# Merging du * B on GpSimd, and moving two pieces of a selective-scan pipeline

## The chip, the cores and the metric

The kernel runs on one core of one Trainium2 chip. The core has five instruction streams that work side by side and meet through semaphores: TensorE (PE; the profile keeps the loading of its stationary operand apart as PEld), VectorE (DVE), ScalarE (ACT), GpSimd (POOL) and SyncE (SP, which issues the DMAs here). The metric is device time in microseconds for one execution of the whole program. A profiled execution also gives the span from the first to the last instruction.

## The reference

Four images of 64 x 64 pixels and 96 channels go through four layers. Layers 0 and 1 are state-space layers and hold nearly all of the time; layers 2 and 3 are linear attention and a quantised feed-forward on the tokens. Layer 1 works on the Fourier transform of the image (33 columns instead of 64). The core of layers 0 and 1 is the same selective scan over four directions, with 16 states for each channel:

```python
def step(hst, inputs):
    ul, dl, bl, cl = inputs
    dA = jnp.exp(dl[..., None] * A)
    hst = hst * dA + (dl * ul)[..., None] * bl[:, :, None, :]
    y = jnp.einsum('bkdn,bkn->bkd', hst, cl)
    return (hst, y)
```

Here `dl` is delta and `dl * ul` is du. For each state n the kernel needs exp(delta * A[n]), the product du * B[n], the running recurrence h, and the sum over n of h * C[n].

## The kernel before

**Tiles.** 128 channels lie on the partitions, and time lies along the free dimension. A layer has three such channel chunks (C = 3). Time is cut into segments of at most 512 columns: eight of 512 in layer 0; 512, 512, 384, 384 and 320 in layer 1. Layer 0 takes two images at once and runs two phases (one for each pair of images) of 4 directions x 8 segments; layer 1 runs four phases (one for each image) of 4 x 5 segments.

**Steps.** A segment is 12 steps: four groups q of four states each, times three chunks c. That makes 2 x 32 x 12 = 768 steps in layer 0 and 4 x 20 x 12 = 960 in layer 1, 1728 in all. One step makes four scans, j = 0 to 3, one for each state of its group. The work is spread over the engines like this:

- For j = 0 and 1 the product du * B is made on ACT in transposed form (bx, L646) and turned by PE into a PSUM bank (`transposed`, L678). The decay exp(delta * A) comes from ACT into SBUF (`front_x`, L682).
- For j = 2 and 3 the product is made on POOL (`front_b`, L700), from du and a tile of B that DMA has spread over the partitions, into places 1 and 2 of a tile h of three states. The decay comes from ACT into a PSUM bank (`front_y`).
- DVE runs the four scans (`scan`, L710). Scan 0 writes into PSUM, over its own input; scans 1 and 2 write into places 0 and 1 of h. Scan 3 writes into place 2 of h, or, in steps whose `kept` holds 3, into PSUM over its decay.
- A state that was kept in PSUM is multiplied by C on DVE into a tile hk (`multiply_kept`, L728), and its last column is put into the state by ACT (`keep_state`, L735). The states in h, two or three, are multiplied by C on POOL in one instruction (`multiply`, L747), after a copy of their last columns (L744).
- PE adds all products into acc, a PSUM bank for each chunk, by transposing them with accumulation (`accumulate`, L757; `add_kept` for hk, `add_rest` for h). After the last group ACT copies acc out (`close_chunk`, L788).

**Order.** The loop over steps writes every engine's order by hand, and each engine runs its own instructions strictly in that order. During step i (called `st`) PE adds the h of step i-2 (`older`), POOL multiplies the h of step i-1 (`before`) and then makes du * B for step i+1 (`nxt`), and PE transposes for step i+1. In `slot` pieces of other work are put in: the preparation of the next segment (`prepare`: projections, delta, du on POOL in L604) and side tasks (projection, convolution, gating, output projection and Fourier transforms of other images; the token layers).

**Buffers that tie the engines.** h has three buffers, so du * B for step i+1 goes into the buffer of step i-2 and waits until PE has added it. The PSUM banks for decays and transposes (`room`) go round by three, in the order: decay 2, decay 3, transposes 0 of the next step, transposes 1 of the next step. So transposes 0 wait for the bank that scan 1 has read, and transposes 1 for the one that scan 2 has read. hk has two buffers, B and C two each.

Of the kernel before, what the change touches and what calls it, by code (L numbers as in the profile page):

```python
# [11 lines left out]
ALU = mybir.AluOpType  # L12
# [10 lines left out]
C, P = 3, 128  # L23
# [7 lines left out]
class Cfg:  # L31
# [5 lines left out]
    def __init__(self, pre, NI, KI, NR, nat, R, parts, rows, segs, eps):  # L37
        self.pre = pre
        self.NI, self.PI, self.KI = NI, P // NI, KI
        self.DI = C * self.PI  # L40
        self.NR, self.L, self.nat = NR, NR * 64, nat
        self.R, self.M = R, R + 2 * NST
        self.parts = parts
        self.rows = [(sum(rows[:i]), n) for i, n in enumerate(rows)]
        self.segs = [(sum(segs[:i]), n) for i, n in enumerate(segs)]
        self.eps = eps
# [466 lines left out]
class Step:  # L513


    def __init__(self, z, q, c):
        self.z, self.q, self.c = z, q, c
        self.nm = f"{z.nm}_{q}_{c}"
        self.kept = (0, 3) if (C * q + c) % (2 * z.cfg.KI) == 1 else (0,)
        self.hk = {}  # L520
        self.px, self.ay = {}, {}


def scans(tc, ctx, phases, ident):
# [8 lines left out]
    nc = tc.nc  # L533
# [96 lines left out]
    def fetch_b(z, q):  # L630
        z.b[q] = broadcast(z, 4 * q + 2, 2, 0)

    def fetch_c(z, q):
        z.c[q] = broadcast(z, 4 * q, 4, 1)

    def make_bx(z, q):

        NI, PI, M, R = z.cfg.NI, z.cfg.PI, z.cfg.M, z.cfg.R
        for j in range(2):
            t = sp.tile([P, NBK, C, P], F32, name=f"bx_{z.nm}_{q}_{j}", tag="bx", bufs=4)  # L640
            z.bx[q, j] = t
            for b, (_, n) in enumerate(z.blocks):
                for i in range(NI):
                    m = i * M + R + 4 * q + j
                    ch = slice(i * PI, (i + 1) * PI)
                    nc.scalar.activation(  # L646
                        t[:n, b, :, ch], z.dut[:n, b, :, ch], AF.Copy, scale=z.bt[:n, b, m : m + 1]
                    )
                    yield
# [15 lines left out]
    def drain(gen):  # L665
        for _ in gen:
            pass
# [3 lines left out]
    def room(st, j):  # L671
        return ps.tile([P, 512], F32, name=f"ab_{st.nm}_{j}", tag=f"ab{next(turn) % 3}")

    def transposed(st, j):

        pb = st.px[j] = room(st, j)
        for b, (t, n) in enumerate(st.z.blocks):
            nc.tensor.transpose(pb[:, t : t + n], st.z.bx[st.q, j][:n, b, st.c], ident[:n, :n])  # L678
# [7 lines left out]
    def front_x(st):  # L686
        st.ax = sp.tile([P, 2, SM], F32, name=f"ax_{st.nm}", tag="ax", bufs=2)
        for j in range(2):
            exp(st.ax[:, j, : st.z.S], st, 4 * st.q + j)
# [5 lines left out]
    def front_b(st):  # L695

        S = st.z.S
        st.h = sp.tile([P, 3, SM], F32, name=f"h_{st.nm}", tag="h", bufs=3)
        for j in range(2):
            nc.gpsimd.tensor_tensor(  # L700
                st.h[:, 1 + j, :S], st.z.du[:, st.c, :S], st.z.b[st.q][:, j, :S], ALU.mult
            )

    def scan(st, j):
        z = st.z
# [43 lines left out]
    def accumulate(st, hc, first=False, last=False):  # L749
        z = st.z  # L750
        if first:
            z.acc[st.c] = ps.tile([P, 512], F32, name=f"acc_{z.nm}_{st.c}", tag=f"acc{st.c}").rearrange(
                "p (b d) -> p b d", b=NBK
            )
        blocks = list(enumerate(z.blocks))
        for b, (t, m) in blocks[:: -1 if last else 1]:
            nc.tensor.matmul(  # L757
                z.acc[st.c][:m, b, :],
                hc[:, t : t + m],
                ident,  # L760
                start=(first and b == 0),
                stop=(last and b == 0),
                is_transpose=True,
            )
# [6 lines left out]
    def add_kept(st, j):  # L771
        accumulate(st, st.hk[j], first=(st.q == 0 and j == 0))
# [26 lines left out]
    with tc.manual_schedule(engines=IN_ORDER):  # L799
        drain(prepare(segs[0]))  # L800
        drain(make_bx(segs[0], 0))
        fetch_b(segs[0], 0)
        fetch_c(segs[0], 0)
        st = steps[0]
        for j in range(2):
            transposed(st, j)
        front_x(st)
        front_b(st)
        before = older = None
        more, pgen, pwants, at, due = Pieces(segs[0], 1, 4), none, None, 0, 0.0  # L810

        def prepare_more(kind):

            nonlocal pwants
            if pwants not in (None, kind):
                return False
            pwants = next(pgen, LATE)
            return True

        def slot(kind, hold=False):  # L820


            nonlocal due
            if hold:
                E.flush()
                return
            prepare_more(kind)
            due = min(due + st.z.ph.rate / 3, 3.0)
            for _ in range(min(int(due), 1 + (due >= 2.0))):
                due -= E.step(kind)  # L830

        def burst():

            if BURST in (pwants, E.wants):
                E.flush()
            if pwants is BURST:
                return prepare_more(BURST)
            if E.wants is BURST:
                E.step(BURST)
                return True  # L840
            return False

        for i, st in enumerate(steps):
            z, q, c, S = st.z, st.q, st.c, st.z.S
            nxt = steps[i + 1] if i + 1 < len(steps) else None
            if q == 0 and c == 0:
                after = z.after
                fresh = at == 0 or z.ph is not segs[at - 1].ph
                if fresh:
                    z.ph.io["y"] = [z.blk.dram_tile(f"y{j}", (2, z.cfg.L, C * P), z.ph.g) for j in range(2)]  # L850
                open_segment(z, segs[at - 1] if at else None)
                if after:
                    E.require(after.ph.needs[after.k % 2])
                pgen, pwants = prepare(after) if after else none, None
                at += 1
            if fresh and q == 0 and c == C - 1:
                for fn, arg in z.ph.side:
                    E.add((fn, arg), fn(E, arg))
            if c == 0:
                if q + 1 < NQ:  # L860
                    fetch_b(z, q + 1)
                elif after:
                    drain(pgen)
                    more = Pieces(after, 0, 4)
                    fetch_b(after, 0)
            if c == 1:
                if q + 1 < NQ:
                    fetch_c(z, q + 1)
                elif after:
                    fetch_c(after, 0)  # L870
            if older:
                add_rest(older)
            if before and 3 in before.kept:
                keep_state(before, 3)
                add_kept(before, 3)
            scan(st, 0)
            front_y(st, 2)
            if nxt:
                front_x(nxt)
            multiply_kept(st, 0)  # L880
            keep_state(st, 0)
            add_kept(st, 0)
            front_y(st, 3)
            long = burst()
            if before:
                multiply(before)
            if nxt:
                front_b(nxt)
            scan(st, 1)
            if nxt:  # L890
                if c == C - 1:
                    drain(more.gen)
                    if q + 2 < NQ:
                        more = Pieces(z, q + 2, 6)
                    elif q + 1 == NQ:
                        more = Pieces(nxt.z, 1, 6)
            slot(None)
            if nxt:
                transposed(nxt, 0)
            more.take(skip=long)  # L900
            scan(st, 2)
            slot(None, hold=long)
            if nxt:
                transposed(nxt, 1)
            if older and older.q == NQ - 1:
                close_chunk(older)
            scan(st, 3)
            if 3 in st.kept:
                multiply_kept(st, 3)
            more.take(skip=long and c == C - 1)  # L910
            slot(LATE)
            older, before = before, st
        multiply(before)
        if 3 in before.kept:
            add_kept(before, 3)
        for st in (older, before):
            add_rest(st)
            close_chunk(st)
        E.finish()
# [704 lines left out]
```

## Time and profile before

| what | value |
|---|---|
| median of 3 runs | 11189.63 us (11177.26 to 11195.26) |
| the profiled execution | 11196.25 us |
| its span | 11194.5 us |
| instructions | 162858 |
| mean granted TensorE clock | 0.901 |
| DMA, read and written | 1215.67 MB and 236.50 MB |

The median and the profiled execution are different runs, so a sum made from the profile's rows belongs to the second and third of these times. A row of the groups gives the line, the engine, the operation, output <- inputs, the shape and the number of instructions; then the busy time in us and the mean duration of one in ns; then the idle time of that engine just before them and what ended it. Lines such as L700 are lines of the kernel before. Names of tiles have their numbers left out: `ab_l` and `b_l` are banks of `room`, `k_l` and `hk_l` are hk, `bc_l` is a spread tile of B or C.

### The profile page before, as it was taken

How to read it: one execution, taken by the hardware profiler on the slowest of the kernel's cores; microseconds unless marked ns; L12 is line 12 of the kernel's file. 1: busy time of each engine (PE TensorE's matmuls, PEld its weight loads, DVE VectorE, ACT ScalarE, POOL GpSimd, SP SyncE). 2: the span in 40 equal slices, each digit the busy share in tenths (PEclk: the TensorE clock that was granted, in tenths of full speed). 3: DMA queues.
4: the chain of work that ended last, by engine and by line, in shares of the span. 5: the costliest groups of instructions: out<-in, count | busy, mean ns of one | idle time of the engine just before them, and what ended most of it. 6: DMA issues, size and time to landing. Idle time of an engine off the chain costs nothing.

```text
span 11194.5 us, 162858 instructions
## 1 busy us (share of the span) xinstructions
PE 8922.4 (80%) x54560; PEld 6578.7 (59%) x54560; DVE 9751.5 (87%) x10419; ACT 9340.7 (83%) x19428; POOL 9616.7 (86%) x7464
## 2 busy tenths in 40 slices
PE   5668788777888888888988888887778877886766
PEld 2555555555667666656775565665556655665554
DVE  5889999889998998999788778988988989889874
ACT  3779999998888998998778878888888888888864
POOL 2999999988888998999789889998988889889870
PEclk8889999889898998999889989998889888999887
DMA  5655554655666546555544444542345322542242
GB/s 145 144 133 124 132 133 121 156 152 150 159 157 136 140 128 149 132 144 161 156 132 130 142 129 128 176 133 88 99 130 146 104 89 97 171 120 93 85 137 44
DMA packets 1204409, 1462.83 MB, mean 131 GB/s; under 512 B 478134, under 2 KB 1017848, under 8 KB 1145072
## 3 DMA queue, kind: packets, MB, share of 16 engines
q1 hardware_dynamic: 1203567, 1452.41, 48.0%
q8 instruction: 431, 7.06, 0.3%
q14 instruction: 411, 3.36, 0.1%
HBM read 1215.67 MB, written 236.50 MB: 130 GB/s over the span
## 4 chain that ended last, share of the span: by engine, by line
POOL 31%; PE 23%; ACT 20%; DVE 16%; issue 7%; DMA 2%; SPq 1%; POOLq 0%; DVEq 0%; ACTq 0%
POOL h_l L747 14%; POOL h_l L700 12%; DVE h_l L710 7%; PE acc_l L757 6%; ACT bx_l L646 4%; ACT ax_l L682 4%; ACT b_l L682 3%; DVE b_l L710 2%; DVE ab_l L710 2%; PE b_l L678 2%; PE pc_l L297 2%; POOL du_l L604 2%; PE pp_l L571 1%; PE pi_l L210 1%; ACT ab_l L682 1%
## 5 line engine op out<-in xcount | busy, mean ns | idle before, releaser
L747 POOL TENSOR_TENSOR h_l<-h_l,bc_l 128x1536 f32<-128x1536 f32 (+2 forms) x1728 | 4783.3, 2768 | 176.1 <-DVE h_l L710 56.1
L700 POOL TENSOR_TENSOR h_l<-du_l,bc_l 128x512 f32<-128x512 f32 (+2 forms) x3456 | 3970.6, 1171 | 582.4 <-PE acc_l L757 552.4
L646 ACT ACTIVATE bx_l<-dut_l,bt_l 128x192 f32<-128x192 f32 (+2 forms) x6272 | 2755.1, 499 | 0.3
L757 PE MATMUL acc_l<-ident,h_l 128*128 128x128 f32 (+1 forms) x16656 | 2427.3, 299 | 293.1 <-POOL h_l L747 291.6
L757 PEld LDWEIGHTS acc_l<-ident,h_l 128*128 128x128 f32 (+1 forms) x16656 | 2129.2, 154 | 901.1 <-POOL h_l L747 469.9
L682 ACT ACTIVATE ax_l<-delta_l,l_alog 128x512 f32<-128x512 f32 (+2 forms) x3456 | 2140.7, 667 | 0.0
L710 DVE TENSOR_TENSOR_SCAN h_l<-b_l,state_l,h_l 128x512 f32<-128x512 f32 (+2 forms) x1386 | 1506.4, 1109 | 132.8 <-ACT b_l L682 113.6
L678 PE MATMUL b_l<-ident,bx_l 128*128 128x128 f32 (+1 forms) x6874 | 1211.8, 295 | 220.4 <-DVE h_l L710 213.4
L682 ACT ACTIVATE b_l<-delta_l,l_alog 128x512 f32<-128x512 f32 (+2 forms) x1968 | 1231.7, 626 | 120.1 <-DVE h_l L710 47.4
L678 PEld LDWEIGHTS b_l<-ident,bx_l 128*128 128x128 f32 (+1 forms) x6874 | 857.1, 149 | 799.9 <-DVE h_l L710 465.8
L710 DVE TENSOR_TENSOR_SCAN b_l<-ax_l,state_l,b_l 128x512 f32<-128x512 f32 (+2 forms) x851 | 965.3, 1134 | 227.8 <-PE b_l L678 225.7
L678 PE MATMUL ab_l<-ident,bx_l 128*128 128x128 f32 x5312 | 888.7, 296 | 228.0 <-DVE h_l L710 220.6
L682 ACT ACTIVATE ab_l<-delta_l,l_alog 128x512 f32<-128x512 f32 x1326 | 913.1, 689 | 178.8 <-DVE h_l L710 91.1
L710 DVE TENSOR_TENSOR_SCAN h_l<-ab_l,state_l,h_l 128x512 f32<-128x512 f32 x803 | 992.4, 1261 | 76.4 <-ACT ab_l L682 41.8
L710 DVE TENSOR_TENSOR_SCAN h_l<-ax_l,state_l,b_l 128x512 f32<-128x512 f32 (+2 forms) x851 | 961.1, 1129 | 55.0 <-PE b_l L678 53.3
L757 PE MATMUL acc_l<-ident,k_l 128*128 128x128 f32 x4757 | 782.2, 293 | 279.3 <-DVE k_l L728 268.5
L678 PEld LDWEIGHTS ab_l<-ident,bx_l 128*128 128x128 f32 x5312 | 650.1, 150 | 591.2 <-DVE h_l L710 423.0
L728 DVE TENSOR_TENSOR k_l<-b_l,bc_l 128x512 f32<-128x512 f32 (+2 forms) x1343 | 831.7, 619 | 46.1
L297 PE MATMUL pc_l<-pad_l,l_dg 128*128 128x512 f32 (+2 forms) x1656 | 789.5, 565 | 62.6 <-ACT uh_l L275 47.0
L757 PE MATMUL acc_l<-ident,hk_l 128*128 128x128 f32 x3628 | 590.4, 297 | 267.7 <-DVE hk_l L728 260.0
L757 PEld LDWEIGHTS acc_l<-ident,k_l 128*128 128x128 f32 x4757 | 584.8, 150 | 369.1 <-DVE k_l L728 311.3
L710 DVE TENSOR_TENSOR_SCAN ab_l<-ax_l,state_l,ab_l 128x512 f32<-128x512 f32 x496 | 631.4, 1273 | 121.4 <-PE ab_l L678 121.1
(252 smaller groups left out, 14330.4 us busy)
## 6 DMA issues: line engine op xcount, KB each, us to landing
bc_l<-l_xd_l SPq DMA_DIRECT2D x640, 512.0 KB
bc_l<-l_xd_l SPq DMA_DIRECT2D x512, 256.0 KB
bc_l<-l_xd_l SPq DMA_DIRECT2D x128, 1024.0 KB
bc_l<-l_xd_l SPq DMA_DIRECT2D x128, 768.0 KB
us_l<-l_u SPq DMA_DIRECT2D x96, 768.0 KB
l_y<-y_l SPq DMA_DIRECT2D x288, 256.0 KB
yt_l<-l_y SPq DMA_DIRECT2D x264, 192.0 KB
yt_l<-l_y SPq DMA_DIRECT2D x128, 384.0 KB
```

The costliest lines, as they stand in the source:

```text
L210: self.nc.tensor.matmul(out[i * cfg.PI : (i + 1) * cfg.PI, :n], wi[:, ki, :], xin[:, max(i, ki), :n], start=(ki == 0), stop=(ki == cfg.KI ...
L297: nc.tensor.matmul(pc[:, : n * 64].rearrange("p (r w) -> p r w", w=64), diag[:, t, :], pad[:, r - p0 + dy : r - p0 + dy + n, dx : dx + 64] ...
L571: nc.tensor.matmul(px[:rows, :S], blk.xpw[:, c, k, :], u[:, c, :S], start=(c == 0), stop=(c == C - 1))
L604: nc.gpsimd.tensor_tensor(z.du[:, c, :S], z.delta[:, c, :S], u[:, c, :S], ALU.mult)
L646: nc.scalar.activation(t[:n, b, :, ch], z.dut[:n, b, :, ch], AF.Copy, scale=z.bt[:n, b, m : m + 1])
L678: nc.tensor.transpose(pb[:, t : t + n], st.z.bx[st.q, j][:n, b, st.c], ident[:n, :n])
L682: nc.scalar.activation(out, z.delta[:, st.c, : z.S], AF.Exp, scale=z.blk.A[:, st.c, z.k, n : n + 1])
L700: nc.gpsimd.tensor_tensor(st.h[:, 1 + j, :S], st.z.du[:, st.c, :S], st.z.b[st.q][:, j, :S], ALU.mult)
L710: nc.vector.tensor_tensor_scan(h[:, ::step], a[:, ::step], b[:, ::step], 0.0 if z.first else z.state[st.c][:, n : n + 1], ALU.mult, ALU.add,)
L728: nc.vector.tensor_tensor(hk[:, : z.S], kept_at(st, j), z.c[st.q][:, j, : z.S], ALU.mult)
L747: nc.gpsimd.tensor_tensor(h, h, z.c[st.q][:, 1 : 1 + m, : z.S], ALU.mult)
L757: nc.tensor.matmul(z.acc[st.c][:m, b, :], hc[:, t : t + m], ident, start=(first and b == 0), stop=(last and b == 0), is_transpose=True,)
```

## The change

Three things change. In `front_b` GpSimd makes du * B of both states with one instruction over 2 x S elements; du is read twice, by a broadcast over the middle dimension. In layer 1 (KI = 2) `kept` holds two states in steps 1 and 7 of 12 instead of steps 1, 5 and 9; in layer 0 (KI = 1) it stays at every second step. And in the loop the call that makes PE add the product of state 0 moves from just behind `keep_state` to behind the first `slot` and the transposes 0 of the next step.

```diff
-        self.kept = (0, 3) if (C * q + c) % (2 * z.cfg.KI) == 1 else (0,)
+        self.kept = (0, 3) if (C * q + c) % (2 if z.cfg.KI == 1 else 6) == 1 else (0,)
...
-        for j in range(2):
-            nc.gpsimd.tensor_tensor(
-                st.h[:, 1 + j, :S], st.z.du[:, st.c, :S], st.z.b[st.q][:, j, :S], ALU.mult
-            )
+        nc.gpsimd.tensor_tensor(
+            st.h[:, 1:, :S],
+            st.z.b[st.q][:, :, :S],
+            st.z.du[:, st.c : st.c + 1, :S].to_broadcast([P, 2, S]),
+            ALU.mult,
+        )
...
             multiply_kept(st, 0)
             keep_state(st, 0)
-            add_kept(st, 0)
             front_y(st, 3)
...
             slot(None)
             if nxt:
                 transposed(nxt, 0)
+            add_kept(st, 0)
             more.take(skip=long)
             scan(st, 2)
```

The arithmetic and the number of PE, DVE-scan and DMA instructions stay as they are.

## The prediction

> **What bounds the kernel now.** I read the busy shares first, then the same shares by stage, then the chain of work that ended last, then the waits, and last the single rows that the change touches.
>
> ```profile
> PE 8922.4 (80%) x54560; PEld 6578.7 (59%) x54560; DVE 9751.5 (87%) x10419; ACT 9340.7 (83%) x19428; POOL 9616.7 (86%) x7464
> ...
> POOL 31%; PE 23%; ACT 20%; DVE 16%; issue 7%; DMA 2%; SPq 1%; POOLq 0%; DVEq 0%; ACTq 0%
> POOL h_l L747 14%; POOL h_l L700 12%; DVE h_l L710 7%; PE acc_l L757 6%; ACT bx_l L646 4%; ACT ax_l L682 4%; ACT b_l L682 3%; DVE b_l L710 2%; DVE ab_l L710 2%; PE b_l L678 2%; PE pc_l L297 2%; POOL du_l L604 2%; PE pp_l L571 1%; PE pi_l L210 1%; ACT ab_l L682 1%
> ```
>
> Four engines lie within seven points, so no one engine is the limit over the whole span. But the chain names GpSimd (POOL) most, and two lines of it make up 26 of its 31 points: the multiplication by C (L747) and du * B (L700). The busy time by stage says where:
>
> ```profile
> core 0: us, PE busy (x) PEld busy (x) DVE busy (x) ACT busy (x) POOL busy (x), PEclk, DMA share, GB/s
> 800.00:2000.00 1200.00, 976.94 (x5728) 689.06 (x5726) 1141.83 (x1089) 1110.42 (x2393) 1173.06 (x869) 0.95 0.52 127
> 2650.00:5150.00 2500.00, 2069.59 (x13060) 1598.29 (x13059) 2326.61 (x2252) 2259.27 (x4851) 2303.98 (x1683) 0.92 0.59 144
> 5150.00:10840.00 5690.00, 4640.57 (x28973) 3442.16 (x28972) 4969.93 (x5667) 4733.36 (x9542) 5016.74 (x4056) 0.90 0.41 124
> ```
>
> From 800 to 2000 us (layer 0, first pair) POOL is busy for 1173 of 1200 us, 97.8%; DVE follows with 95.2%, ACT with 92.5%. In the second pair DVE and POOL are level (93.1 and 92.2%). In layer 1 POOL has 88.2, DVE 87.3, ACT 83.2 and PE 81.6%: there short stretches alternate, some held by POOL, some by PE's side work. The waits that the change could touch:
>
> ```profile
> POOL h_l L700 <- PE acc_l L757: 552.4, 306, 7.7
> DVE b_l L710 <- PE b_l L678: 284.4, 242, 6.5
> DVE ab_l L710 <- PE ab_l L678: 147.7, 94, 6.6
> DVE h_l L710 <- POOL h_l L700: 61.9, 58, 9.1
> ```
>
> The columns are us in total, times, and longest. POOL waits for PE because du * B reuses the buffer of h three steps back, which PE must have added up. DVE waits 432 us, in 336 of 1728 steps, for the transposes that scan 0 reads, and only 62 us for du * B.
>
> **Part 1, one instruction for du * B: -78 us.** It removes one of two POOL instructions in each of 1728 steps; the elements stay. The shapes of the new instruction stand in the trace already, as C products of two states:
>
> ```profile
> L700 POOL TENSOR_TENSOR h_l<-du_l,bc_l 128x512 f32<-128x512 f32 x2304 | 2892.9, 1278 | 281.0 <-PE acc_l L757 268.1 <-issue 8.5 <-POOL h_l L747 3.0
> L747 POOL TENSOR_TENSOR h_l<-h_l,bc_l 128x1536 f32<-128x1536 f32 x672 | 2320.0, 3452 | 75.4 <-DVE h_l L710 26.9 <-DVE qb L1189 2.9 <-PE pp_l L612 0.6
> L747 POOL TENSOR_TENSOR h_l<-h_l,bc_l 128x1024 f32<-128x1024 f32 x480 | 1135.4, 2365 | 38.3 <-DVE h_l L710 5.6
> ...
> L1355 POOL TENSOR_TENSOR y<-y,kb 128x384 f16<-128x384 f16 x48 | 44.3, 923 | 2.7 <-ACT y L1352 2.6
> L1359 POOL TENSOR_TENSOR tok<-tok,y 128x384 f32<-128x384 f32 x48 | 44.0, 917 | 3.8
> ```
>
> By durations the saving is 2 x 1278 - 2365 = 191 ns a step. But instructions that follow each other overlap, as their starts show:
>
> ```profile
> 1402.11 2.51 POOL L700 TENSOR_TENSOR h_l<-du_l,bc_l 128x512 f32<-128x512 f32 x2
> 1404.57 2.39 POOL L747 TENSOR_TENSOR h_l<-h_l,bc_l 128x1024 f32<-128x1024 f32 x1
> 1406.90 2.52 POOL L700 TENSOR_TENSOR h_l<-du_l,bc_l 128x512 f32<-128x512 f32 x2
> 1409.58 3.46 POOL L747 TENSOR_TENSOR h_l<-h_l,bc_l 128x1536 f32<-128x1536 f32 x1
> ```
>
> From start to start the pair takes 1404.57 - 1402.11 = 2.46 us and the one of 1024 takes 1406.90 - 1404.57 = 2.33: 0.13. By busy time over count the pair is 2 x 2892.9/2304 = 2.51 and the one 1135.4/480 = 2.365: 0.146. I take 0.145, which over 1728 steps is 251 us of POOL (330 by durations, 225 by starts).
>
> The Trainium skill (Perfetto Trace Analysis, section GPSIMD Engine Instruction) says not to trust a GpSimd span and to time such instructions by the spacing of their starts. It speaks against the 191 ns, and the rows above agree with it; by its way of counting alone the gross saving would be about 225 us in place of 251.
>
> That du is read twice with a step of zero is new for f32. The nearest rows are L1355, whose second operand is broadcast over its middle dimension, and L1359, whose is not: 923 and 917 ns for 384 elements. So I take nothing for it, with 0.7% of 2.365 us x 1728 = +29 us as the upper bound and -29 as the lower. The wait for h's buffer is the same one as before; behind it stands the next C product, as now. What is late: scan 2 may now start only when both halves are there, 2.33 us after the start in place of about 1.24 (below).
>
> Only time on the path counts. L700 holds 12% of the chain, 1343 us; 0.145 of about 2.49 us is 5.8%: -78 us. That is allowed by the next engine: in the stage from 800 to 2000 us a step takes 6.05 us (198.5 steps by L700's count), so POOL falls by 2.4 points to 95.4%, just above DVE's 95.2.
>
> **Part 2, the second PSUM state in layer 1 in one step of six: +14 us.** Of 12 steps of a segment two instead of three keep state 3 in PSUM. That is one step in each of 16 x 5 = 80 segments (32 of 512 columns, 32 of 384, 16 of 320). There DVE loses a multiplication (rows of L728: 691, 557, 491 ns): 32 x 0.691 + 32 x 0.557 + 16 x 0.491 = 47.8 us. POOL's C product grows from two states to three: 3452 - 2365 = 1087 ns, 2635 - 1818 = 817, 2224 - 1544 = 680, so 34.8 + 26.1 + 10.9 = 71.8 us. ACT loses 64 copies of a state column of 146 ns, 9 us. POOL's own copy takes 190 ns for two columns and for three; scans into SBUF and into PSUM take the same (1259 and 1271 ns); PE adds as many blocks. Put on the path by chain shares: POOL +71.8/4783.3 = 1.5% of L747's 14% (1567 us) = +24; DVE -47.8 x 16% = -8; ACT -9 x 20% = -2.
>
> **Part 3, the product of state 0 added after the first transposes: -10 us.** Only PE's order changes: from [add hk0, side work, transposes 0, transposes 1] to [side work, transposes 0, add hk0, transposes 1]. Transposes 0 need the buffer that scan 1 frees; hk0 is ready one scan earlier. When PE runs with DVE, it will stand still during scan 1 (1.2 us from start to start), where it adds hk0 now in 0.66 us (timeline at 5810 to 5813 us), and will have 0.66 + 0.66 us to do under scan 2, which lasts 1.27 us. So transposes 1, which need the end of scan 2, come at most 0.05 us later; scan 2 is the cover. Were it gone, the sums behind would be 0.6 us late, and du * B's 306 waits for them longer by 184 us in all. When PE is late, transposes 0 come up to 0.66 us sooner: at most 336 x 0.66 = 222 us of DVE's 432. But where PE is late the chain mostly stays on PE, whose work is the same, and the L678 transposes hold only 2% of it. I take -10, near no gain, and keep +60 (a third of the 184) and -200 as ends.
>
> **The sum.** -78 + 24 - 8 - 2 - 10 = -74. The profiled run took 11196.25 us, its span is 11194.5; 11196 - 74 = 11122. The median of the runs, 11189.6, lies 6.6 below the profiled run, so the forecast is 11116 us (-0.66%).
>
> **Rivals.** (a) DVE or PE takes over at once. For it: DVE at 95% beside POOL in layer 0, and 93.1 against 92.2 in the second pair. Against it: DVE waits there too, and those waits end on POOL's or PE's late work. Then part 1 gives back all but some 20 us, part 2's POOL cost stays covered: about 11185, no change. (b) The order pays: if two thirds of 222 us come through, 148, with the -64 of the rest: 11190 - 64 - 148 = about 10980. For it: 432 us are DVE's largest wait. Against it: the 2% of the chain. (c) Slower: scan 2 waits for the whole fused instruction. Where POOL is 97% busy (72 of the 50 us windows of the span, about 600 steps) the wait would be 2.33 - 1.24 = 1.09 us longer. It decides if the delay comes back to POOL, whose next C product needs scan 3: from 74/1.09 = 68 such steps on the path on it eats the gain. If a quarter of the 600 do, +163 - 74 = +89: about 11280. Against it: scans 2 and 3 take 2.5 us, and between a du * B and the C product of its step POOL has another C product (2.33 to 3.45 us) and another du * B (2.33) to do, 4.7 to 5.8 us; so 2 us and more are spare, and only 58 waits are there now. (d) The change does less than it says, if the broadcast is not one pass: POOL's busy time would not fall, part 2 would stay, and the time be 11190 + 14 - 10, again no change.
>
> **Chances.** Forecast (11050 to 11165) 0.50; (b) 0.20; (a) and (d) together 0.16; (c) 0.14. A measurement of this kernel tells about 0.2% (22 us) from no change. Faster by more: 0.50 + 0.20 = 0.70; within: 0.16; slower: 0.14. The range reaches down to (b) with the lower bounds of the rest, 10960, and up a little into (c), 11235; its own range for the forecast alone is 11050 to 11165.
>
> **What would show it.** Part 1: du * B as 1728 instructions of about 2365 ns at 512 columns, and POOL's busy time lower by about 251 - 72 = 180 us, near 9440. Part 2: 800 C products of three states instead of 720 in layer 1 and a shorter L728. Part 3: DVE's 432 us on the transposes falls; du * B's 552 us on PE does not grow. (c) shows as DVE waiting for du * B far over 62 us. The prediction is wrong if POOL's busy time falls as said and the span doesn't, or if an f32 broadcast runs at another rate.

## The result, and the profile after

The changed kernel takes 11136.12 us (median of 5; 11125.66 to 11141.0) against 11177.26 us for the kernel before on the same chip (11168.12 to 11195.26): a ratio of 0.9959, 95% interval 0.9945 to 0.9974. A second measurement, made beside the later experiments, gave 0.9951 (0.9938 to 0.9963). So it is faster by 0.4 to 0.5%, some 41 to 50 us, where the forecast had 74.

The busy shares of the changed kernel, from its page:

```profile
span 11139.2 us, 159640 instructions
...
PE 8763.9 (79%) x54560; PEld 6560.6 (59%) x54560; DVE 9707.0 (87%) x10339; ACT 9325.5 (84%) x19364; POOL 9444.0 (85%) x5736
```

POOL has 1728 instructions fewer and 9616.7 - 9444.0 = 173 us less to do; the forecast had about 180. DVE lost 44.5 us (forecast 47.8). The span lost 55 us. Two of the new rows of POOL, with shapes kept apart:

```profile
L699 POOL TENSOR_TENSOR h_l<-bc_l,du_l 128x1024 f32<-128x1024 f32 x1152 | 2725.8, 2366 | 303.3 <-PE acc_l L759 289.4 <-issue 6.7 <-POOL h_l L749 5.0
L749 POOL TENSOR_TENSOR h_l<-h_l,bc_l 128x1024 f32<-128x1024 f32 x448 | 1059.2, 2364 | 35.9 <-DVE h_l L712 5.1
```

The du * B of two states takes 2366 ns, the C product of two states 2364: reading du twice with a step of zero costs nothing. The rows of the whole span's waits that bear on the change (others are left out):

```profile
POOL h_l L699 <- PE acc_l L759: 552.2, 326, 8.0
POOL state_l L746 <- DVE h_l L712: 308.4, 241, 10.7
DVE b_l L712 <- PE b_l L678: 211.2, 208, 5.8
DVE h_l L712 <- PE b_l L678: 107.5, 130, 3.9
DVE h_l L712 <- POOL h_l L699: 101.0, 122, 9.5
DVE ab_l L712 <- PE ab_l L678: 97.4, 59, 9.0
DVE h_l L712 <- PE ab_l L678: 40.6, 38, 5.3
```

DVE's waits for transposes 0 (out is a bank, `b_l` or `ab_l`) fell from 432 to 309 us, those for transposes 1 (out is h) rose from 67.6 + 18.8 = 86 to 148. POOL's wait for PE did not move (552), but POOL now waits 308 us for DVE's last scan, where it waited 234. POOL stands idle some 118 us longer than before (173 us less work in 55 us less span), and 75 of them are this wait for DVE. The same stage that the prediction leaned on, in the changed kernel:

```profile
core 0: us, PE busy (x) PEld busy (x) DVE busy (x) ACT busy (x) POOL busy (x), PEclk, DMA share, GB/s
800.00:2000.00 1200.00, 963.66 (x5711) 689.30 (x5708) 1138.57 (x1087) 1111.01 (x2390) 1141.44 (x667) 0.95 0.53 128
```

POOL's busy time fell from 97.8 to 95.1%, as forecast, but only 197 C products (one in each step) start in this stretch, where 199 did before. DVE's share stayed at 95% (1141.83 before, 1138.57 after).

To place the gain I took from each trace the start of the first C product, of the 769th (the first of layer 1) and of the last. They give the length of the two layers in one profiled execution, as differences to the kernel before (4915 us and 5693 us):

| kernel | layer 0 | layer 1 |
|---|---|---|
| changed kernel, first profile | +14 | -67 |
| changed kernel, second profile | -7 | -52 |
| du * B fused alone | -15 | -32 |
| fewer kept steps alone | 0 | +9 |
| later add alone | +18 | -26 |
| fused, later add | +1 | -66 |
| fused, fewer kept | -16 | -50 |
| all, later add in layer 1 only | -23 | -65 |
| all, later add in layer 0 only | -2 | -37 |
| the same as the last but one, and 5 of 12 kept in layer 0 | -43 | -64 |

The two profiles of the changed kernel differ by 15 to 21 us in a layer, so a single figure here says little. Three pairs of rows differ by the fusing alone (fused against the kernel before, "fused, later add" against "later add alone", "fused, fewer kept" against "fewer kept steps alone"): it shortens layer 0 by 15 to 17 us in all three, and layer 1 by 32, 40 and 59. The rows together also suggest that the later add lengthens layer 0 and shortens layer 1, which the later experiments were made to test.

### The profile page after: what moved, and what is told of

It reads as the page before. It is cut to its first block, busy times and chain, and to the rows that moved or that the text cites. A ratio compares the mean times of both kernels' runs of the same rounds, so it can differ in the third digit from the quotient of the medians.

```text
span 11139.2 us, 159640 instructions
## 1 busy us (share of the span) xinstructions
PE 8763.9 (79%) x54560; PEld 6560.6 (59%) x54560; DVE 9707.0 (87%) x10339; ACT 9325.5 (84%) x19364; POOL 9444.0 (85%) x5736
## 4 chain that ended last, share of the span: by engine, by line
PE 16%; POOL 13%; ACT 10%; DVE 9%; issue 4%; DMA 1%; SPq 0%; POOLq 0%; DVEq 0%; ACTq 0%
POOL h_l L749 7%; POOL h_l L699 5%; PE acc_l L759 4%; DVE h_l L712 4%; ACT ax_l L682 2%; PE b_l L678 2%; ACT bx_l L646 1%; ACT b_l L682 1%; DVE ab_l L712 1%; PE pc_l L297 1%; POOL du_l L604 1%; PE piv L1129 1%; PE pp_l L571 1%; PE pp_l L581 1%; PE ab_l L678 1%
## 5 line engine op out<-in xcount | busy, mean ns | idle before, releaser
L749 POOL TENSOR_TENSOR h_l<-h_l,bc_l 128x1536 f32<-128x1536 f32 (+2 forms) x1728 | 4853.6, 2809 | 194.4 <-DVE h_l L712 56.7
L699 POOL TENSOR_TENSOR h_l<-bc_l,du_l 128x1024 f32<-128x1024 f32 (+2 forms) x1728 | 3720.9, 2153 | 597.1 <-PE acc_l L759 552.2
L678 PE MATMUL b_l<-ident,bx_l 128*128 128x128 f32 (+1 forms) x6816 | 1240.3, 297 | 509.1 <-DVE h_l L712 495.3
L678 PE MATMUL ab_l<-ident,bx_l 128*128 128x128 f32 x5424 | 943.8, 301 | 531.7 <-DVE h_l L712 511.8
L678 PEld LDWEIGHTS ab_l<-ident,bx_l 128*128 128x128 f32 x5424 | 674.5, 152 | 924.9 <-DVE h_l L712 753.7
L712 DVE TENSOR_TENSOR_SCAN h_l<-ab_l,state_l,h_l 128x512 f32<-128x512 f32 x849 | 1049.7, 1263 | 99.8 <-POOL h_l L699 56.6
L730 DVE TENSOR_TENSOR k_l<-b_l,bc_l 128x512 f32<-128x512 f32 (+2 forms) x1291 | 801.3, 621 | 65.8 <-DMA bc_l<-l_xd_l 0.8
L759 PE MATMUL acc_l<-ident,k_l 128*128 128x128 f32 (+1 forms) x4580 | 780.3, 291 | 6.1 <-DVE k_l L730 4.9
L712 DVE TENSOR_TENSOR_SCAN h_l<-ax_l,state_l,ab_l 128x512 f32<-128x512 f32 x510 | 648.6, 1272 | 30.9 <-PE ab_l L678 30.1
L730 DVE TENSOR_TENSOR hk_l<-ab_l,bc_l 128x512 f32<-128x512 f32 x896 | 619.8, 692 | 51.5 <-DMA bc_l<-l_xd_l 5.4
```

The lines of the kernel that those rows point to most:

```text
L699: nc.gpsimd.tensor_tensor(st.h[:, 1:, :S], st.z.b[st.q][:, :, :S], st.z.du[:, st.c : st.c + 1, :S].to_broadcast([P, 2, S]), ALU.mult,)
L712: nc.vector.tensor_tensor_scan(h[:, ::step], a[:, ::step], b[:, ::step], 0.0 if z.first else z.state[st.c][:, n : n + 1], ALU.mult, ALU.add,)
L730: nc.vector.tensor_tensor(hk[:, : z.S], kept_at(st, j), z.c[st.q][:, j, : z.S], ALU.mult)
L749: nc.gpsimd.tensor_tensor(h, h, z.c[st.q][:, 1 : 1 + m, : z.S], ALU.mult)
L759: nc.tensor.matmul(z.acc[st.c][:m, b, :], hc[:, t : t + m], ident, start=(first and b == 0), stop=(last and b == 0), is_transpose=True,)
```

## The experiments

All ratios are against the kernel before on the same chip, in five rounds. The first four kernels take the change apart.

**Only du * B fused.**

```diff
-        for j in range(2):
-            nc.gpsimd.tensor_tensor(
-                st.h[:, 1 + j, :S], st.z.du[:, st.c, :S], st.z.b[st.q][:, j, :S], ALU.mult
-            )
+        nc.gpsimd.tensor_tensor(
+            st.h[:, 1:, :S],
+            st.z.b[st.q][:, :, :S],
+            st.z.du[:, st.c : st.c + 1, :S].to_broadcast([P, 2, S]),
+            ALU.mult,
+        )
```

> The kernel before with only du * B as one instruction. Theory (POOL's time counts with its share of the chain): 251 us less of POOL, about -78 us, ratio 0.993; POOL's busy time about 250 us lower. Rival A (the gain of the change came from the order of PE's adds): less than 20 us, ratio 0.998 to 1.000. Rival B (scan 2 pays for waiting for the whole instruction): DVE's wait for du * B grows from 62 us to over 200, and the time rises.

Measured: 11145.1 us against 11185.75, ratio 0.9962 (0.995 to 0.9975), -41 us. POOL's busy time in its page is 9374.0 us, 243 lower (expected 250). So the fusing is as large on POOL as forecast and gives about half of the 78 us. Its gain can't be told from that of the whole change (0.9959 and 0.9951), so rival A falls. Rival B falls too: DVE waits 79.6 us for du * B.

**Only fewer kept steps in layer 1.**

```diff
-        self.kept = (0, 3) if (C * q + c) % (2 * z.cfg.KI) == 1 else (0,)
+        self.kept = (0, 3) if (C * q + c) % (2 if z.cfg.KI == 1 else 6) == 1 else (0,)
```

> The kernel before with only layer 1 changed to two PSUM states in one step of six. Theory: POOL +72 us, DVE -48 us, at their chain shares +14 us, ratio 1.001. Rival A (DVE is the tighter of the two in layer 1): up to -40 us, ratio 0.996. Rival B (POOL's extra time counts in full): +72 us, ratio 1.006.

Measured: 11202.32 us against 11185.75, ratio 1.0019 (1.0009 to 1.0029): +17 us between the medians, +21 by the ratio. That is the theory's sign and about its size (+14), and both rivals lie outside.

**Only the later add.**

```diff
-            add_kept(st, 0)
             front_y(st, 3)
...
                 transposed(nxt, 0)
+            add_kept(st, 0)
```

> The kernel before with only the add of state 0's product moved behind the transposes 0. Theory: -10 us, ratio 0.999; DVE's waits for transposes 0 fall from 432 to about 310 us, those for transposes 1 rise from 86 to about 140. Rival A (the order makes most of the gain): -40 us or more, ratio 0.996. Rival B (PE standing still during scan 1 costs more than it brings): +20 us or more, with more of POOL's waits for PE.

Measured: ratio 1.0001 (0.9992 to 1.001). The waits moved the way that was expected, to 216.8 + 117.8 = 335 us for transposes 0 and 103.8 + 39.7 = 144 for transposes 1, and the time did not.

**The two du * B in the opposite order.**

```diff
-        for j in range(2):
+        for j in (1, 0):
             nc.gpsimd.tensor_tensor(
```

> The kernel before with its two du * B instructions in the opposite order, so that scan 2 gets its operand one instruction (1.24 us) later and POOL's time stays. It prices the later operand alone. Theory (two us and more are spare): no change, ratio 0.999 to 1.001, though DVE's named wait for du * B grows from 62 us. Rival (scan 2's later start is on the path and is what ate part of the gain): +30 us or more, ratio 1.003.

Measured: ratio 1.0002 (0.9993 to 1.0011). DVE's wait for du * B, in the waits of this kernel, nearly doubled against the 61.9 us before, and cost nothing:

```profile
DVE h_l L710 <- POOL h_l L700: 119.3, 103, 10.7
```

So the later operand is not on the path: rival (c) of the prediction is out.

The next four say how the parts act together, and what POOL's time is worth.

**Fused, with the later add, kept as before.** The edits of the first and the third kernel.

> du * B as one instruction and the later add of state 0's product, with layer 1's three kept steps of 12 as before. Alone the first took 41 us off and the second nothing. Theory (the order pays only once POOL is not the engine that ends last): beyond the sum, -55 us or more, ratio 0.995 or lower. Rival (the parts just add up): -41 us, ratio 0.9963.

**Fused, with fewer kept steps, the old order of adds.** The edits of the first and the second.

> du * B as one instruction and two PSUM states in one step of six, with PE's order as before. Alone they gave -41 and +21 us. Theory (their terms add, since both are POOL time): -20 us, ratio 0.998. Rival (once POOL is relieved, DVE's 48 us less pay and POOL's 72 us more are covered): -45 us or more, ratio 0.996 or lower.

**The changed kernel with more POOL time.**

```diff
+    spare = sp.tile([P, 64], F32, name="spare", tag="spare")
...
+        nc.gpsimd.memset(spare[:, :64], 0.0)
```

(The memset stands behind du * B.)

> The changed kernel with a GpSimd memset of 128x64 on a tile that nobody reads behind each du * B: about as much POOL time as the fusing took out (some 0.15 us in each of 1728 steps, 250 us), and no wait for another engine. Theory (only POOL's time counts, at the slope that the fusing alone showed, 41 of 251): +41 us against the changed kernel, so about -5 against the kernel before, ratio 0.9995. Rival A (the chain's share of 31% is the slope): +78 us, ratio 1.003. Rival B (the gain lies in fewer instructions and semaphores, not in POOL's time): no change against the changed kernel, ratio 0.996.

**The changed kernel again.**

> The changed kernel itself on this chip, so that the parts can be compared with it: ratio 0.996, the same for every theory.

Measured, all four on one chip: 0.9952 (0.9939 to 0.9964), 0.9945 (0.9932 to 0.9957), 0.9987 (0.9978 to 0.9996) and 0.9951 (0.9938 to 0.9963). The first, the second and the changed kernel can't be told apart. The first lies between its theory (0.995) and its rival (0.9963), and its interval holds both. The second is its rival: the kept steps, which cost 0.19% alone, show no cost once du * B is fused (0.9952 without and 0.9951 with them), so POOL's 72 us more are covered; that DVE's 48 us pay beyond that is not shown. The later add does nothing for the whole time, in either setting, that clears the intervals.

The memset took POOL time without a wait for another engine, and the groups show how much:

```profile
L707 POOL MEMSET spare<- 128x64 f32 x1728 | 265.4, 154 | 0.0
```

Its duration is 154 ns, but POOL's busy time rose only by 9584.7 - 9444.0 = 141 us, as the next instruction starts before it ends. The time rose by 34 us (11168.64 against 11134.27, intervals apart). The slope, that is the time gained or lost for each us of an engine's work, is 34/141 = 0.24; by the ends of the ratios' intervals it may be anything from 0.12 to 0.46. The fusing alone had 41/243 = 0.17 (0.12 to 0.23). So POOL's time counts and rival B falls. The fusing's slope stays under the 0.31 of the chain; the memset's, by itself, doesn't exclude it.

The next two follow the signs by layer.

**The later add in layer 1 only**, otherwise the changed kernel.

```diff
             keep_state(st, 0)
+            if z.cfg.KI == 1:
+                add_kept(st, 0)
             front_y(st, 3)
...
                 transposed(nxt, 0)
-            add_kept(st, 0)
+            if z.cfg.KI == 2:
+                add_kept(st, 0)
```

> The changed kernel with the later add of state 0's product in layer 1 only; in layer 0 it stands where it stood before. In the single profiles the later add made layer 0 some 10 to 30 us longer and layer 1 some 10 to 30 us shorter. Theory (the two effects are real and have opposite signs): -65 us or more against the kernel before, ratio 0.994 or lower, below the changed kernel (0.9951 to 0.9959) and below the one with fusing and fewer kept steps but the old order (0.9945). Rival (the stage differences are the scatter of single profiles): the same as those, 0.995.

**The later add in layer 0 only**: the same with 1 and 2 exchanged.

> The opposite: the later add in layer 0 only. Theory: the worst of the four orders, -30 us, ratio 0.997. Rival (scatter): 0.995 as all the others.

Measured: 0.9933 (0.992 to 0.9947) and 0.9964 (0.9951 to 0.9976; expected 0.997), on one chip. The two intervals lie apart, so the place of the later add matters by layer: its cost in layer 0 and its pay in layer 1 make some 34 us together. Each sign by itself rests on comparisons with the changed kernel and with the old order in both layers, whose intervals overlap, though all lean the same way. The first is -75 us where -65 or more was expected, and the lowest of the four orders.

DVE's waits say the same by layer. From the kernel with the old order (fused, fewer kept) to the changed one, its wait for transposes 0 goes from 117 to 91 us in layer 0 and that for transposes 1 from 29 to 53 (windows 230 to 5120 us), which cancels; in layer 1 (5160 to 10760 us) it is 281 to 218 against 58 to 96, which leaves 25 us gained.

What may cost in layer 0 shows in DVE's instructions. First the kernel with the old order (fused, fewer kept), one step after a step with two kept states; then the changed kernel at the same place. Columns: start, length, then the instruction.

```profile
1415.47 1.27 DVE L712 TENSOR_TENSOR_SCAN ab_l<-ab_l,state_l,h_l 128x512 f32<-128x512 f32 x1
1416.77 0.69 DVE L730 TENSOR_TENSOR hk_l<-ab_l,bc_l 128x512 f32<-128x512 f32 x1
1417.38 1.28 DVE L712 TENSOR_TENSOR_SCAN ab_l<-ax_l,state_l,ab_l 128x512 f32<-128x512 f32 x1
1418.70 0.69 DVE L730 TENSOR_TENSOR hk_l<-ab_l,bc_l 128x512 f32<-128x512 f32 x1
```

```profile
1419.58 1.26 DVE L712 TENSOR_TENSOR_SCAN ab_l<-ab_l,state_l,h_l 128x512 f32<-128x512 f32 x1
1420.88 0.69 DVE L730 TENSOR_TENSOR hk_l<-ab_l,bc_l 128x512 f32<-128x512 f32 x1
1421.48 1.28 DVE L712 TENSOR_TENSOR_SCAN ab_l<-ax_l,state_l,ab_l 128x512 f32<-128x512 f32 x1
1422.86 0.69 DVE L730 TENSOR_TENSOR hk_l<-ab_l,bc_l 128x512 f32<-128x512 f32 x1
```

From scan 0 to the product of its state it is 1418.70 - 1417.38 = 1.32 us with the old order and 1422.86 - 1421.48 = 1.38 with the new. This is one of many: from the starts in the traces, over the 369 of layer 0's 384 such steps with no other instruction between, the median is 1.31 us with the old order and 1.38 with the new. The same goes by layer in the two kernels above: 1.31 in the layer with the old order, 1.38 in the other. The view by line, from 300 to 5100 us, counts the separate semaphore instructions on DVE's queue for the products (count, then shortest, median and longest in ns), old order first:

```profile
L730 DVEq EVENT_SEMAPHORE  x250: 49/50/7817, 314.0 to 5080.3; - x125
```

```profile
L730 DVEq EVENT_SEMAPHORE  x622: 21/21/3412, 305.9 to 5093.7; - x156
```

372 more, about one for each of layer 0's 384 kept steps. The code says why. hk has two buffers, so after a kept step the product of state 0 takes the buffer that the last step's state 0 had. With the old order PE added that buffer ahead of transposes 0, which scan 0 waits for anyway; with the new one the add stands behind them and DVE has to wait for it separately. 0.07 us x 384 = 27 us is about what the later add seems to cost in layer 0: from the changed kernel to the one with the later add in layer 1 only the ratio falls by 0.0018 to 0.0026, 20 to 29 us. The gap and the count are shown; that they are what costs there is argued, since the next run puts as much into every step and costs no more. A third buffer of hk, which should take the wait away, was not tried. In layer 1 the same happens in 64 steps, and DVE's shorter wait for transposes 0 outweighs it.

The last two ask what DVE's time is worth.

**The changed kernel with more DVE time.** (The tile `spare` is made as above.)

```diff
             scan(st, 1)
+            nc.vector.memset(spare[:, :64], 0.0)
```

> The changed kernel with a DVE memset of 128x64 on a tile that nobody reads behind scan 1 of every step, some 0.08 to 0.13 us in each of 1728. Theory (DVE holds layer 0 now and shares layer 1, so its time counts at a higher slope than GpSimd's): of some 170 us more DVE time half or more is seen, +85 us or more against the changed kernel, ratio 1.003 against the kernel before, and in layer 0 nearly all of it. Rival (no engine holds layer 0, DVE's slope is the same small one that GpSimd shows): +35 us, ratio 0.9985.

Measured: 0.9968 (0.9957 to 0.998), 0.0009 to 0.0017 above the two measurements of the changed kernel, 10 to 19 us, with intervals that overlap. DVE's busy time rose by only 9766.2 - 9707.0 = 59 us, but that understates the probe. From scan 1 to scan 2 of 512 columns, start to start, it is 1.262 us with the memset and 1.188 without (medians): 0.074 us, and 128 us over 1728 steps. Half of that would be 64 us, ratio about 1.001, outside the interval. So the theory that DVE's time counts at half or more did not hold, and the rival's small slope fits better: 0.08 to 0.15 by these figures. The memset stands right ahead of scan 2, where DVE sometimes waits in any case, so this is the price of DVE's time at that place.

**Fewer kept steps in layer 0 too**, with the later add in layer 1 only. (Only the condition in `kept` is shown.)

```diff
-(C * q + c) % (2 if z.cfg.KI == 1 else 6) == 1
+(C * q + c) in ((1, 3, 6, 8, 11) if z.cfg.KI == 1 else (1, 7))
```

> The kernel with the later add in layer 1 only, and in layer 0 two states in PSUM in 5 of 12 steps instead of 6 (64 steps in all). That moves 64 x 0.691 = 44 us off DVE and puts 64 x 1.087 = 70 us on GpSimd, in layer 0 alone. Theory (DVE holds layer 0, and GpSimd has room there since the fusing): -10 to -30 us against the same kernel with 6 of 12. Rival (GpSimd holds layer 0 still): +20 us or more against it.

Measured: 11095.93 us against 11191.11, ratio 0.9916 (0.9903 to 0.993): 20 us below the same kernel with 6 of 12, and the lowest of all. Its page:

```profile
PE 8845.8 (80%) x54560; PEld 6575.1 (59%) x54560; DVE 9658.3 (87%) x10275; ACT 9312.4 (84%) x19308; POOL 9513.1 (86%) x5736
```

DVE has 9704.0 - 9658.3 = 46 us less, POOL 9513.1 - 9449.3 = 64 us more, and layer 0 is 20 us shorter in the profile. The theory's -10 to -30 came, and the rival's +20 did not: more POOL time and less DVE time did not make layer 0 slower, so POOL has room there after the fusing. That DVE's time is what paid is not shown: the intervals of the two kernels overlap in part, the kept steps also stand in another pattern, and the memset just before found DVE's time nearly free.

## Why the prediction was right, and where its terms were off

**Direction and rows were right.** The forecast of 11116 us missed by 20, inside its own range. The broadcast costs nothing, the instruction takes 2366 ns for 2365 forecast, and the 0.145 us for the fused pair, taken between starts and durations, gave 243 us measured for 251. The 330 us by durations would have been wrong. The Trainium skill's rule (Perfetto Trace Analysis, section GPSIMD Engine Instruction) is to go by the spacing of starts and not by spans; the 225 us that the prediction drew from it lie nearer to the 243 than the 330 do.

**Part 1 was mis-sized: -78 forecast, -41 measured.** The step that failed is the price of POOL's time: "Only time on the path counts", with L700's 12% of the chain as the share that pays, and the check behind it, "That is allowed by the next engine". POOL at 97.8% and DVE at 95.2 from 800 to 2000 us were read as room for all of the 2.4 points. In the kernel that only fuses, the same stretch shows how little came through (columns as above):

```profile
800.00:2000.00 1200.00, 972.18 (x5748) 683.48 (x5747) 1146.70 (x1094) 1119.42 (x2405) 1149.39 (x672) 0.96 0.52 128
```

POOL fell by 2.0 points to 95.8%, but DVE got only 0.4% more done in the 1200 us, 1146.70 for 1141.83. In the kernel before, two steps of that stretch on DVE:

```profile
1705.63 1.27 DVE L710 TENSOR_TENSOR_SCAN h_l<-ax_l,state_l,b_l 128x512 f32<-128x512 f32 x1
1706.82 2.43 DVE L710 TENSOR_TENSOR_SCAN h_l<-b_l,state_l,h_l 128x512 f32<-128x512 f32 x2
1709.17 1.26 DVE L710 TENSOR_TENSOR_SCAN b_l<-ax_l,state_l,b_l 128x512 f32<-128x512 f32 x1
1710.46 0.69 DVE L728 TENSOR_TENSOR k_l<-b_l,bc_l 128x512 f32<-128x512 f32 x1
1711.07 1.27 DVE L710 TENSOR_TENSOR_SCAN h_l<-ax_l,state_l,b_l 128x512 f32<-128x512 f32 x1
1712.26 1.26 DVE L710 TENSOR_TENSOR_SCAN h_l<-b_l,state_l,h_l 128x512 f32<-128x512 f32 x1
1713.43 1.26 DVE L710 TENSOR_TENSOR_SCAN b_l<-b_l,state_l,h_l 128x512 f32<-128x512 f32 x1
1714.73 0.69 DVE L728 TENSOR_TENSOR k_l<-b_l,bc_l 128x512 f32<-128x512 f32 x1
1715.34 1.28 DVE L710 TENSOR_TENSOR_SCAN b_l<-ax_l,state_l,b_l 128x512 f32<-128x512 f32 x1
1716.65 0.69 DVE L728 TENSOR_TENSOR k_l<-b_l,bc_l 128x512 f32<-128x512 f32 x1
1717.26 1.27 DVE L710 TENSOR_TENSOR_SCAN h_l<-ax_l,state_l,b_l 128x512 f32<-128x512 f32 x1
```

Here DVE stands back to back: two steps in 1717.26 - 1705.63 = 11.63 us, 5.82 a step, where the mean of the stage is 6.05. The gaps ahead of the three products, 0.1 us of the 11.63, count as idle but belong to its work. They are one point of the five that DVE's share lacks; most of the rest is waits. POOL ran as full beside it, but in this stage the waits of the kernel before show that DVE hardly waited for it directly:

```profile
PE acc_l L757 <- POOL h_l L747: 29.0, 21, 3.3
...
DVE ab_l L710 <- PE ab_l L678: 14.4, 7, 2.7
DVE h_l L710 <- ACT ab_l L682: 13.9, 8, 3.4
...
DVE b_l L710 <- PE b_l L678: 6.7, 7, 2.2
...
DVE h_l L710 <- POOL h_l L700: 1.1, 2, 0.5
...
DVE ab_l L710 <- POOL h_l L747: 0.7, 2, 0.6
```

Of DVE's 58 us idle in this stage, all rows together, 22.5 end on PE, 20.5 on ACT and 1.8 on POOL. The fused instruction does nothing for the work of PE and ACT. Some of these waits may still go back to POOL, since PE waited 29.0 us for POOL's products, so they don't prove how much POOL held.

The sizes by layer are firmer. At the forecast's price layer 0, with 768 of the 1728 fused instructions, would have gained 35 us and layer 1 43. The three pairs of profiles gave 15 to 17 in layer 0 and 32 to 59 in layer 1, so the shortfall lies mostly in layer 0. The 31% of the chain is one way back through work that is nearly level on several engines, and here it promised more than the fusing paid: a slope of 0.17, with 0.24 for the memset on POOL. Rival (a), "DVE or PE takes over at once", was half right: in layer 0 more than half of the forecast gain did not come. Which engine took over there is open: the run with one more shift from DVE to POOL in layer 0 fits DVE, and the memset on DVE speaks against it.

**Part 2: +14 forecast, +21 alone.** But beside the fusing no cost is seen. The terms were added as if each kept its slope; the fusing gave POOL the room that covers part 2's 72 us. Two errors of the sum, part 1 too large by 37 and part 2 charged where it was covered, partly cancel: so far the forecast's nearness is luck, and the measured gain is 41 to 50 us of the 74.

**Part 3: -10 forecast, about 0.** The cover named, scan 2, holds: transposes 1 are waited for a little more, transposes 0 less, as forecast. Not foreseen were the opposite signs in the two layers and the separate wait on DVE, which the prediction's list of added waits lacks; rival (b), two thirds of 222 us, is out, as the runs with and without the later add differ by less than their intervals.

**Rival (c)** was taken out by the swapped order, **(d)** by POOL's busy time. The windows of 50 us with POOL at 97% or more, which size rival (c), are 85 in the trace and not 72; nothing else hangs on that count.

## What to carry to other kernels

A high busy share shows an engine to be full, not that others wait for it: before crediting a stage to its fullest engine, read in that stage alone who waits for it, and look at the runner-up's instructions from start to start. Don't take an engine's share of the chain for what its time will pay. A filler instruction prices it, at the place where it stands, if the filler's own cost is taken from start to start and not from busy time. After relieving one engine, moves of load onto it that used to cost can become free, so try them again, and by stage: the kernel with the later add in layer 1 only and one more shift from DVE to GpSimd in layer 0 nearly doubled the gain of the change, 0.84% for 0.41 to 0.49. When PE's order is changed, ask which semaphore waits were covered by the old order: here an instruction moved behind the transposes that DVE waits for anyway needed a wait of its own.

## What was not expected of the hardware

The added wait ahead of DVE's product made that place 0.07 us longer (1.31 to 1.38 us in the median). It is not the separate instruction as such. In about a third of those steps it stands ahead of scan 0 and not of the product, and the product is late all the same (1.37). In the kernel before, scans of 512 columns in layer 0 that follow a scan start 1.18 to 1.19 us after it (medians), with none, one or two such instructions ahead. A short filler costs less than its duration: a DVE memset of 112 ns added 0.07 us from one scan's start to the next, though DVE's busy time shows only half of that, and a GpSimd memset of 154 ns added 141/1728 = 0.08 us.
